# The units of the attention's key tiles as one stream, with one exponential over two units

## The chip, the cores and the metric

The kernel runs on one core of a Trainium2 chip. Its engines are TensorE (PE; its weight loads are listed as PEld), VectorE (DVE), ScalarE (ACT), GpSimd (POOL) and SyncE (SP, which issues DMAs). Each takes its instructions in the order of its own queue and waits for the others through semaphores. PE writes into eight PSUM banks of 128 x 512 fp32 elements; DVE and ACT read them, POOL works in SBUF. The metric is the device time of one launch in microseconds (us), the median of several runs.

## The reference

The input is four images of 128 channels and 64 x 64 positions. A first layer (convolution, state-space scan, norms) is added to it; then each image becomes 4,096 tokens of 128 channels, which go through an additive attention and a recurrent layer. Only the attention is touched here:

```python
q = jnp.einsum('bld,ud->blu', x, Wt)                     # U = 32
k = jnp.einsum('bld,ud->blu', x, Wx)
beta = jnp.tanh(q[:, :, None, :] + k[:, None, :, :] + bh)
alpha = jnp.einsum('bsju,u->bsj', beta, Wa[:, 0]) + ba[0]
alpha = jax.nn.softmax(jnp.tanh(alpha), axis=-1)
c_r = jnp.einsum('bsj,bjd->bsd', alpha, x)               # added to the tokens
```

For each of 4 x 4,096 queries and 4,096 keys this is a sum of 32 hyperbolic tangents, weighted by `Wa`.

## The kernel before

The kernel has three stages: `_layer0`, `_rational` (the attention) and `_chunked` (the recurrent layer). A fourth, `_general`, is entered only if a test on the device fails. All that follows is in `_rational`, whose instructions stand on the engines' queues in the order in which the Python code emits them.

A sum of several tanh terms is a ratio of two sums over sign patterns: with m terms there are 2^m patterns, each an exponential of a signed sum of q's, times one of k's. The 32 terms are split into groups of 6, 6, 5, 5, 5 and 5, so the patterns take 64 + 64 + 32 + 32 + 32 + 32 rows. `F` holds the keys' exponentials (two layers of 128 rows, 4,096 keys), `E` the queries' (512 at a time), and `cE` the queries' times the weights. A denominator is a product of `F` with `E`, a numerator one of `F` with `cE`, each contracting the 64 or 32 rows of its group. A tile of 128 keys and 512 queries so needs six ratios; they are made in three units of two:

- unit A: layer 0, rows 0 to 63 and 64 to 127
- unit B1: layer 1, rows 0 to 31 and 32 to 63
- unit B2: layer 1, rows 64 to 95 and 96 to 127

`products` (L1201) writes a unit's two denominators (`lower`, L1209) into a tile `pd` of two banks, its two numerators (`upper`, L1214) into two tiles `pn` of one bank. There are two `pd` (four banks), three `pn` and one `ct`. In the trace every fp32 product is two passes of a matmul, so it counts as two.

The loop is over four images and eight query blocks of 512 each, 32 blocks in all, and inside over 32 key tiles `jt`. Per tile:

- `inverse` (L1221), ACT: a Ln of the 1,024 denominators (L1223), then an Exp of the negative (L1224), which gives the reciprocals in `ra` (unit A) or `rb` (B1, B2)
- `times` (L1217), DVE: the two halves multiplied by the numerators, from PSUM (L1219)
- POOL: the ratios of B1 added to those of A (L1338), and those of B2 (L1325)
- DVE: the two halves added into `A[:, jt, :]` (L1335)

The order on PE is by hand (L1315 to L1342): denominators of A, numerators of B2 of the tile before beside denominators of B1, numerators of A, denominators of B2 beside numerators of B1. B2's multiplication, its addition and the sum into `A` come one tile late.

After the 32 tiles ACT applies tanh and exp to `A` in four parts (L1373, L1374). Meanwhile the next block's tile 0 is made with DVE's reciprocal instead of ACT (`ahead`, L1355, and `direct`, L1227); so the loop of all blocks but the first starts with tile 1. `weighted` (L1349) multiplies `A` by the transposed tokens `xT` into the bank `ct`; the products of tiles 0 to 19 come at once, those of the last twelve are put between tiles 2 to 13 of the next block. `closing` (L1235) divides and stores: `take`, `den`, four reciprocals and `end`, at the tiles of `CLOSE_AT`. The table `between` also holds the norm of the next image (`NORM_AT`), the next queries (`QUERIES_AT`) and, at an image's start, the transposes `turn`. The keys of the next image are made at the end of an image (L1382).

Of the kernel before, what the change touches and what calls it, by code (L numbers as in the profile page):

```python
# [8 lines left out]
F32 = mybir.dt.float32  # L9
AF = mybir.ActivationFunctionType  # L10
# [5 lines left out]
P = 128  # L16
# [22 lines left out]
WARM = 16  # L39
QB = 512  # L40
PARTS = ((0, 4), (4, 12), (12, 20), (20, 32))
CLOSE_AT = (14, 16, 17, 18, 19, 20, 21)
NORM_AT = (15, 17, 19, 20)
QUERIES_AT = (23, 25)
NOW = 20
REACH = 21.0
LOWER = 2.0**-13
# [1001 lines left out]
def _rational(ctx, tc, k, x1, x2, top, Wt, Wx, bh, Wa, ba):  # L1049
# [11 lines left out]
    one = ctx.enter_context(tc.tile_pool(name="none", bufs=1))  # L1061
    two = ctx.enter_context(tc.tile_pool(name="ntwo", bufs=2))
    sb = ctx.enter_context(tc.tile_pool(name="nsb", bufs=2))
    ra = ctx.enter_context(tc.tile_pool(name="nra", bufs=3))
    rb = ctx.enter_context(tc.tile_pool(name="nrb", bufs=4))
    psD = ctx.enter_context(tc.tile_pool(name="npsD", bufs=2, space=PSUM))
    psN = ctx.enter_context(tc.tile_pool(name="npsN", bufs=3, space=PSUM))
    psW = ctx.enter_context(tc.tile_pool(name="npsW", bufs=1, space=PSUM))
# [7 lines left out]
    def pn():  # L1076
        return psN.tile([P, QB], F32, name="pn", tag="pn")
# [57 lines left out]
    def exponent(ps, w, src, i, out, bias=0.0):  # L1135

        nc.tensor.matmul(ps, w[:, i * P : (i + 1) * P], src, start=True, stop=True)  # L1137
        nc.scalar.activation(out, ps, AF.Exp, bias=bias)
        n = next(tops)
        nc.vector.tensor_reduce(top[:, n : n + 1], ps, AX.X, ALU.max)  # L1140


    def norm_load(b, xn, cols):
        nc.sync.dma_start(xn[:, cols], x1[b, :, cols])

    def norm_steps(xn, cols, alloc):

        xc = xn[:, cols]
        n = cols.stop - cols.start
        held = {}  # L1150

        def centre():
            ps = alloc()
            _mm(nc, ps, k.avg, xc, n)
            nc.vector.tensor_tensor(xc, xc, ps, ALU.subtract)

        def square():
            held["sq"] = rb.tile([P, CH], F32, name="sq", tag="rb")[:, 0:n]
            nc.scalar.activation(held["sq"], xc, AF.Square)

        def rate():
            ps = alloc()
            _mm(nc, ps, k.avg, held["sq"], n)
            _rsqrt(nc, held["sq"], ps, k.eps5)

        def scale():
            nc.gpsimd.tensor_tensor(xc, xc, held["sq"], ALU.mult)

        return centre, square, rate, scale

    def keys(F, xn, c, ps, i):

        exponent(ps, w_k, xn[:, blocks[c]], i, F[:, i, blocks[c]], b_k[:, i : i + 1])

    def turn(xT, xn, c):

# [34 lines left out]
        products((ps[:, 0, :], ps[:, 1, :]), unit, F, jt, E)  # L1211
        return ps

    def upper(unit, F, jt, cE):  # L1214
        return products((pn(), pn()), unit, F, jt, cE)

    def times(r, ns):  # L1217
        for a in range(2):
            nc.vector.tensor_tensor(r[:, a, :], r[:, a, :], ns[a], ALU.mult)  # L1219

    def inverse(d, pool, tag):  # L1221
        r = pool.tile([P, 2, QB], F32, name=tag, tag=tag)
        nc.scalar.activation(r, d, AF.Ln, scale=LOWER)  # L1223
        nc.scalar.activation(r, r, AF.Exp, scale=-1.0)  # L1224
        return r

    def direct(d, ns, pool, tag):  # L1227

        r = pool.tile([P, 2, QB], F32, name=tag, tag=tag)
        for a in range(2):  # L1230
            nc.vector.reciprocal(r[:, a, :], d[:, a, :])  # L1231
            nc.vector.scalar_tensor_tensor(r[:, a, :], r[:, a, :], 1.0 / LOWER, ns[a], ALU.mult, ALU.mult)
        return r

    def closing(b, s, ct, xr, parts):  # L1235

        held = {}

        def take():
            held["ct"] = one.tile([P, QB], F32, name="ct_s")  # L1240
            nc.vector.tensor_copy(held["ct"], ct)

        def denominators():
            held["den"] = pw()
            nc.tensor.matmul(held["den"], den_w, held["ct"], start=True, stop=True)
            held["rec"] = one.tile([P, QB], F32, name="rec")

        def invert(i):
            cols = slice(i * QB // parts, (i + 1) * QB // parts)
            nc.vector.reciprocal(held["rec"][:, cols], held["den"][:, cols])  # L1250

        def end():
            num = pn()
            nc.tensor.matmul(num, fix, held["ct"], start=True, stop=True)
            nc.vector.tensor_tensor(held["rec"], held["rec"], num, ALU.mult)
            nc.gpsimd.tensor_tensor(xr, xr, held["rec"], ALU.add)
            nc.sync.dma_start(x2[b, :, blocks[s]], xr)

        return [take, denominators] + [lambda i=i: invert(i) for i in range(parts)] + [end]


    nn = L // CH
    xn = two.tile([P, L], F32, name="xn")
    for c in range(nn):
        norm_load(0, xn, slice(c * CH, (c + 1) * CH))
    ln_exp()
    todo = [
        norm_steps(xn, slice(c * CH, (c + 1) * CH), lambda: pd().rearrange("p a q -> p (a q)")) for c in range(nn)
    ]
    for i in range(nn + 1):  # L1270
        for d, c in ((0, i), (1, i), (2, i - 1), (3, i - 1)):
            if 0 <= c < nn:
                todo[c][d]()
    F = big.tile([P, 2, L], F32, name="F")
    xT = big.tile([P, JT, P], F32, name="xT")
# [16 lines left out]
    for b in range(B):  # L1292
        upcoming = None
        for s in range(nq):
# [16 lines left out]
                        lambda i=i, s=s, of=of, E_next=E_next: queries(E_next, of, (s + 1) % nq, i)  # L1311
                    )
            ln_exp()
            late = None
            for jt in range(start, JT + 1):  # L1315
                if jt < JT:
                    dA = lower("A", F, jt, E) if jt > start else first[0]
                if late is not None:
                    pj, rA_, rB2_ = late
                    nB2 = upper("B2", F, pj, cE)  # L1320
                if jt < JT:
                    dB1 = lower("B1", F, jt, E) if jt > start else first[1]
                if late is not None:
                    times(rB2_, nB2)
                    nc.gpsimd.tensor_tensor(rA_, rA_, rB2_, ALU.add)  # L1325
                if jt < JT:
                    nA = upper("A", F, jt, cE)
                    rA = inverse(dA, ra, "ra")
                    times(rA, nA)
                    dB2 = lower("B2", F, jt, E)  # L1330
                    nB1 = upper("B1", F, jt, cE)
                    rB1 = inverse(dB1, rb, "rb")
                    times(rB1, nB1)
                if late is not None:
                    nc.vector.tensor_tensor(A[:, pj, :], rA_[:, 0, :], rA_[:, 1, :], ALU.add)  # L1335
                if jt == JT:
                    break
                nc.gpsimd.tensor_tensor(rA, rA, rB1, ALU.add)  # L1338
                rB2 = inverse(dB2, rb, "rb")
                late = jt, rA, rB2  # L1340
                for go in between.pop(jt, ()):
                    go()  # L1342

            if more:
                E, cE = E_next, weigh(E_next)
# [9 lines left out]
            def ahead(step):  # L1355
                if not more:
                    return
                if step == 0:
                    held["A"], held["B1"] = lower("A", F, 0, E), lower("B1", F, 0, E)
                    held["A"] = direct(held["A"], upper("A", F, 0, cE), ra, "ra")  # L1360
                elif step == 1:
                    held["B2"] = lower("B2", F, 0, E)
                    held["B1"] = direct(held["B1"], upper("B1", F, 0, cE), rb, "rb")
                    nc.gpsimd.tensor_tensor(held["A"], held["A"], held["B1"], ALU.add)
                elif step == 2:
                    held["first"] = lower("A", F, 1, E)
                    r = direct(held["B2"], upper("B2", F, 0, cE), rb, "rb")
                    nc.gpsimd.tensor_tensor(held["A"], held["A"], r, ALU.add)
                else:
                    held["first"] = held["first"], lower("B1", F, 1, E)  # L1370

            for i, (lo, hi) in enumerate(PARTS):
                nc.scalar.activation(A[:, lo:hi, :], A[:, lo:hi, :], AF.Tanh, bias=b_a)  # L1373
                nc.scalar.activation(A[:, lo:hi, :], A[:, lo:hi, :], AF.Exp)  # L1374
                if i == 0:
                    if turned:

                        F = big.tile([P, 2, L], F32, name="F")
                        for c in range(nq):
                            ps = pd()  # L1380
                            for a in range(2):
                                keys(F, upcoming, c, ps[:, a, :], a)  # L1382
                    ahead(0)
                if hi <= NOW or not more:
                    for jt in range(lo, hi):
                        weighted(jt)
                ahead(i + 1) if i + 1 < len(PARTS) else None
            if more:
                nc.vector.tensor_tensor(A[:, 0, :], held["A"][:, 0, :], held["A"][:, 1, :], ALU.add)
                first = held["first"]  # L1390
                start = 1
            between = {}
# [207 lines left out]
```

## Time and profile before

| | |
|---|---|
| median of three runs | 11853.89 us (11846.7 to 11861.68) |
| profiled execution | 11853.99 us |
| its span, first to last instruction | 11852.3 us |
| PE, DVE, ACT, POOL busy in the span | 88%, 78%, 80%, 73% |
| instructions of the attention | from 4071 to 11550 us |
| one query block without a change of image (6189.3 to 6417.9) | 228.6 us; ACT busy 221.3, PE 222.6, DVE 171.7, POOL 162.5 |
| one with a change of image (5926.4 to 6189.3) | 262.9 us; ACT busy 232.6 |
| Ln of 1,024 columns from PSUM | 1.01 to 1.03 us |
| Exp of 1,024 columns in SBUF | 1.06 us |
| multiplication, 512 columns (L1219) | 0.68 us |
| POOL's additions, 1,024 columns (L1325, L1338) | 2.37 and 2.65 us |

A row of the page's groups, or of the trace's, gives the source line, the engine, the tile written and the tiles read, the shape, the count, the busy time and the mean in nanoseconds; behind the second bar stands how long the engine was idle just before these instructions and what ended most of that. A row of the timeline gives start and duration; rows that follow each other on an engine are merged and counted. A busy PE is not one at its peak: its matmuls overlap, and their ends are modelled.

### The profile page before, as it was taken

Reading aid. Unit: us, or ns where it says so; the run is one execution under the profiler, and the core shown is the slowest. Engines: PE = TensorE matmul, PEld = TensorE weight load, DVE = VectorE, ACT = ScalarE, POOL = GpSimd, SP = SyncE. Lnnn points to the kernel's source line nnn. Section 1 sums busy time; section 2 is a strip of 40 time slices with the busy share of each in tenths; the row PEclk is TensorE's granted clock in tenths of the full one; section 3 lists DMA queues with packets and bytes.
Section 4 is the critical chain, followed back from the end, with each engine's and each line's share of the span. In section 5 each row is a group of like instructions: output and inputs, shape, how many; then the busy total and the mean of one; then the engine's idle time right before and its main releaser. Section 6 shows DMA issues by size and latency. Waiting matters only on the chain.

```text
span 11852.3 us, 111573 instructions
## 1 busy us (share of the span) xinstructions
PE 10379.5 (88%) x36083; PEld 3211.2 (27%) x36083; DVE 9191.1 (78%) x10131; ACT 9444.7 (80%) x10096; POOL 8602.6 (73%) x3648
## 2 busy tenths in 40 slices
PE   6687787678677699999999999999999999999996
PEld 2121122122111133333333333323333323333324
DVE  4999899899989677777777777777777767777763
ACT  3455555655555599999989999989999989999985
POOL 2899889889889677677757776767677667767761
PEclk8898898899888799999999999999999999999998
DMA  4778778778778300000000000000000000000001
GB/s 105 181 178 197 170 173 190 177 174 189 176 170 182 78 1 6 3 3 3 6 3 3 3 6 3 3 6 3 3 3 6 3 2 2 4 2 2 4 15 46
DMA packets 224900, 737.81 MB, mean 62 GB/s; under 512 B 41057, under 2 KB 42017, under 8 KB 223793
## 3 DMA queue, kind: packets, MB, share of 16 engines
q1 hardware_dynamic: 221184, 729.96, 26.1%
q8 instruction: 284, 4.65, 0.2%
q14 instruction: 312, 2.55, 0.1%
q10 hardware_dynamic: 3120, 0.64, 0.0%
HBM read 613.01 MB, written 117.44 MB: 62 GB/s over the span
## 4 chain that ended last, share of the span: by engine, by line
PE 48%; ACT 11%; DVE 4%; issue 3%; POOL 2%; DMA 0%; POOLq 0%; DVEq 0%; SPq 0%; ACTq 0%
PE pn L1204 25%; PE pd L1204 15%; ACT A L1373 4%; PE ct L1349 3%; ACT A L1374 2%; DVE rb L1219 1%; ACT rb L1223 1%; ACT rb L1224 1%; PE ct L1137 1%; DVE A L1335 1%; ACT ra L1223 1%; POOL ra L1338 1%; POOL ra L1325 1%; PE wxs L1492 0%; PE pd L1137 0%
## 5 line engine op out<-in xcount | busy, mean ns | idle before, releaser
L1204 PE MATMUL pn<-cE,F 32*128 32x512 f32 (+1 forms) x12288 | 4740.0, 651 | 174.3 <-DVE cE L1192 58.0
L1219 DVE TENSOR_TENSOR rb<-rb,pn 128x512 f32<-128x512 f32 x3972 | 2546.0, 682 | 1310.2 <-PE pd L1204 683.5
L1204 PE MATMUL pd<-E,F 32*128 32x512 f32 (+1 forms) x12288 | 3507.2, 654 | 33.8 <-DVE ra L1231 32.2
L1338 POOL TENSOR_TENSOR ra<-ra,rb 128x1024 f32<-128x1024 f32 x993 | 2634.6, 2653 | 960.3 <-DVE rb L1219 960.3
L1325 POOL TENSOR_TENSOR ra<-ra,rb 128x1024 f32<-128x1024 f32 x993 | 2348.5, 2365 | 381.1 <-DVE rb L1219 320.3
L629 POOL TENSOR_TENSOR dBu<-dtdu,bbcc 128x1024 f32<-128x1024 f32 x1024 | 2397.6, 2366 | 276.6 <-DMA dtdu<-ddd 158.4
L1224 ACT ACTIVATE rb<-rb 128x1024 f32<-128x1024 f32 x1986 | 2103.2, 1059 | 62.8
L1204 PEld LDWEIGHTS pn<-cE,F 32*128 32x128 f32 (+1 forms) x12288 | 1424.6, 185 | 2560.7 <-DVE rb L1219 995.7
L1223 ACT ACTIVATE rb<-pd 128x1024 f32<-128x1024 f32 x1986 | 2009.0, 1012 | 100.5 <-PE pn L1204 87.7
L671 PE MATMUL py<-h,gather 128*32 128x512 f32 x4096 | 1298.7, 698 | 478.2 <-POOL h L654 381.5
L1219 DVE TENSOR_TENSOR ra<-ra,pn 128x512 f32<-128x512 f32 x1986 | 1316.5, 684 | 234.6 <-ACT ra L1224 196.8
L1204 PEld LDWEIGHTS pd<-E,F 32*128 32x128 f32 (+1 forms) x12288 | 936.5, 186 | 1673.6 <-issue 751.2
L624 ACT ACTIVATE pa<-dtdu,a_neg 128x1024 f32<-128x1024 f32 x1024 | 1147.2, 1120 | 52.2 <-DVE h L644 31.3
L654 POOL TENSOR_TENSOR h<-h,bbcc 128x1024 f32<-128x1024 f32 x384 | 923.0, 2404 | 343.3 <-ACT carry L652 336.7
L644 DVE TENSOR_TENSOR_SCAN pa<-pa,carry,dBu 128x1024 f32<-128x1024 f32 x480 | 1125.8, 2345 | 22.3 <-ACT pa L624 11.3
L1224 ACT ACTIVATE ra<-ra 128x1024 f32<-128x1024 f32 x993 | 1050.9, 1058 | 31.4
L1349 PE MATMUL ct<-A,xT 128*128 128x512 f32 x2048 | 1037.1, 633 | 10.3 <-ACT A L1374 10.1
L1223 ACT ACTIVATE ra<-pd 128x1024 f32<-128x1024 f32 x993 | 1010.0, 1017 | 44.1 <-PE pd L1204 10.7
L652 ACT COPY carry<-pa 128x1 f32<-128x1 f32 x640 | 103.6, 162 | 1118.3 <-DVE h L651 1116.5
L1335 DVE TENSOR_TENSOR A<-ra 128x512 f32<-128x512 f32 x993 | 749.8, 755 | 114.6 <-POOL ra L1325 114.6
L651 DVE TENSOR_TENSOR h<-pa,bbcc 128x1024 f32<-128x1024 f32 x640 | 784.1, 1225 | 60.4 <-DVE pa L644 1.8
L644 DVE TENSOR_TENSOR_SCAN h<-pa,carry,dBu 128x1024 f32<-128x1024 f32 x288 | 675.1, 2344 | 115.4 <-PE py L671 70.7
(286 smaller groups left out, 8847.9 us busy)
## 6 DMA issues: line engine op xcount, KB each, us to landing
bbcc<-bcd SPq DMA_DIRECT2D x1024, 256.0 KB, 7.0
dtdu<-ddd SPq DMA_DIRECT2D x1024, 256.0 KB, 7.1
ddd<-dd SPq DMA_DIRECT2D x64, 1024.0 KB, 5.1
src<-src SPq DMA_DIRECT2D x64, 512.0 KB, 8.3
xs<-in_x_dram SPq DMA_DIRECT2D x16, 512.0 KB, 7.6
src<-xs SPq DMA_DIRECT2D x16, 512.0 KB, 3.0
bcd<-bc SPq DMA_DIRECT2D x64, 128.0 KB, 2.0
src<-xsT SPq DMA_DIRECT2D x16, 512.0 KB, 4.4
```

What stands on the lines that cost most here:

```text
L624: nc.scalar.activation(dA, its[m].DT[r][:, 0, :], AF.Exp, scale=a)
L629: nc.gpsimd.tensor_tensor(dBu, its[m].DT[r][:, 1, :], its[m].BC[q][:, 0, :], ALU.mult)
L644: nc.vector.tensor_tensor_scan(to[:, step], dA[:, step], live.pop(("dBu", u))[:, step], 0.0 if m % nch == 0 else its[m - 1].carry[:, col : ...
L654: nc.gpsimd.tensor_tensor(h, h, cc, ALU.mult)
L671: nc.tensor.matmul(it.y[to, c], gather, live["h", v][:, c], start=False, stop=(q == QS - 1))
L1204: nc.tensor.matmul(ps[a], F[lo:hi, i, jt * P : (jt + 1) * P], side[lo:hi, i, :], start=True, stop=True)
L1219: nc.vector.tensor_tensor(r[:, a, :], r[:, a, :], ns[a], ALU.mult)
L1223: nc.scalar.activation(r, d, AF.Ln, scale=LOWER)
L1224: nc.scalar.activation(r, r, AF.Exp, scale=-1.0)
L1325: nc.gpsimd.tensor_tensor(rA_, rA_, rB2_, ALU.add)
L1338: nc.gpsimd.tensor_tensor(rA, rA, rB1, ALU.add)
L1349: nc.tensor.matmul(ct, xT[:, jt, :], A[:, jt, :], start=(jt == 0), stop=(jt == JT - 1))
```

## The change

The tiles' units become one stream: `units` lists A, B1, B2 of all the block's tiles, and a loop takes two of them at a time, without regard to where a tile ends. The two share a buffer `r` of 2,048 columns: each has its own Ln, and one Exp covers both. `upper` makes one half of a unit's numerators at a time, into one bank. On PE the numerators of the units in hand alternate with the denominators of the units four and five places ahead. On DVE, a sum into `A` stands between two multiplications; on POOL, the additions of the pair follow each other. What is in `between` for a tile is emitted in the round before the one that holds the tile's B2.

Besides: the keys of a new image are made by `all_keys`, two products, then two Exps, then two maxima; the first norms work on 512 columns in `pn` banks; the squares of the norm have their own two buffers; the last product of `closing` uses the `ct` bank; and two positions in `CLOSE_AT` and `QUERIES_AT` move by one tile. The pools `ra` (3) and `rb` (4), of 1,024 columns, give way to `rr` (4), of 2,048.

```diff
-CLOSE_AT = (14, 16, 17, 18, 19, 20, 21)
+CLOSE_AT = (14, 16, 17, 18, 19, 20, 22)
-QUERIES_AT = (23, 25)
+QUERIES_AT = (24, 26)
...
-    ra = ctx.enter_context(tc.tile_pool(name="nra", bufs=3))
-    rb = ctx.enter_context(tc.tile_pool(name="nrb", bufs=4))
+    rr = ctx.enter_context(tc.tile_pool(name="nrr", bufs=4))
...
+    def all_keys(F, xn, c):
+        ps = pd()
+        for i in range(2):
+            nc.tensor.matmul(ps[:, i, :], w_k[:, i * P : (i + 1) * P], xn[:, blocks[c]], start=True, stop=True)
+        for i in range(2):
+            nc.scalar.activation(F[:, i, blocks[c]], ps[:, i, :], AF.Exp, bias=b_k[:, i : i + 1])
+        for i in range(2):
+            n = next(tops)
+            nc.vector.tensor_reduce(top[:, n : n + 1], ps[:, i, :], AX.X, ALU.max)
...
-    def upper(unit, F, jt, cE):
-        return products((pn(), pn()), unit, F, jt, cE)
+    def upper(unit, F, jt, cE, half):
+        ps = pn()
+        i, parts = groups[unit]
+        lo, hi = parts[half]
+        nc.tensor.matmul(ps, F[lo:hi, i, jt * P : (jt + 1) * P], cE[lo:hi, i, :], start=True, stop=True)
+        return ps
...
         def end():
-            num = pn()
+            num = pw()
...
-            late = None
-            for jt in range(start, JT + 1):
...
+            units = [(jt, unit) for jt in range(start, JT) for unit in ("A", "B1", "B2")]
+            den, num, ratio = dict(enumerate(first)), {}, {}
+            sums = []
...
+            def inverses(u):
+                pair = [v for v in (u, u + 1) if v < len(units)]
+                if not pair:
+                    return
+                r = rr.tile([P, 2, 2, QB], F32, name="r")
+                for i, v in enumerate(pair):
+                    ratio[v] = r[:, i]
+                    nc.scalar.activation(r[:, i], den.pop(v), AF.Ln, scale=LOWER)
+                n = len(pair)
+                nc.scalar.activation(r[:, 0:n], r[:, 0:n], AF.Exp, scale=-1.0)
+
+            def times(u, half):
+                if u < len(units):
+                    r = ratio[u][:, half, :]
+                    nc.vector.tensor_tensor(r, r, num.pop((u, half)), ALU.mult)
+
+            def added(u):
+                if u >= len(units) or units[u][1] == "A":
+                    return
+                to = ratio[u - (1 if units[u][1] == "B1" else 2)]
+                nc.gpsimd.tensor_tensor(to, to, ratio[u], ALU.add)
+                if units[u][1] == "B2":
+                    sums.append((units[u][0], to))
+
+            def summed():
+                for jt, r in sums:
+                    nc.vector.tensor_tensor(A[:, jt, :], r[:, 0, :], r[:, 1, :], ALU.add)
+                sums.clear()
+
+            inverses(0)
+            numerators(0, 0)
+            numerators(0, 1)
+            denominators(2)
+            numerators(1, 0)
+            denominators(3)
+            for u in range(0, len(units), 2):
+                inverses(u + 2)
+                times(u, 0)
+                numerators(u + 1, 1)
+                denominators(u + 4)
+                times(u, 1)
+                numerators(u + 2, 0)
+                denominators(u + 5)
+                times(u + 1, 0)
+                numerators(u + 2, 1)
+                summed()
+                times(u + 1, 1)
+                added(u)
+                added(u + 1)
+                for v in (u + 2, u + 3):
+                    if v < len(units) and units[v][1] == "B2":
+                        for go in between.pop(units[v][0], ()):
+                            go()
+                numerators(u + 3, 0)
+            summed()
```

`denominators(u)` calls `lower`, and `numerators(u, half)` calls `upper`, for the unit `u` of the stream if there is one.

## The prediction

> **What bounds the kernel now.** I read the page first (busy shares, slices, the chain that ended last), then the stage of the change by windows, by form, and instruction by instruction.
>
> ```profile
> span 11852.3 us, 111573 instructions
> ACT  3455555655555599999989999989999989999985
> PE 48%; ACT 11%; DVE 4%; issue 3%; POOL 2%; DMA 0%; POOLq 0%; DVEq 0%; SPq 0%; ACTq 0%
> ```
>
> ```profile
> 6189.30:6417.90 228.60, 222.62 (x845) 69.86 (x844) 171.66 (x241) 221.26 (x202) 162.47 (x67) 0.97 0.01 4
> ```
>
> The span stands against the profiled execution's own 11853.99 us, 0.1 above the median of the runs, 11853.89. The slices show ACT at 8 to 9 tenths in the attention alone; in the chain PE leads. The last line is one of 32 query blocks (PE, PEld, DVE, ACT, POOL busy): PE and ACT are both near 97%, so the profile of busy time cannot say which sets the pace. The order of single instructions can:
>
> ```profile
> 6000.30 1.12 PE L1349 MATMUL ct<-A,xT 128*128 128x512 f32 x2
> ...
> 6001.35 1.13 PE L1204 MATMUL pd<-E,F 64*128 64x512 f32 x4
> ...
> 6002.41 0.70 PE L1204 MATMUL pn<-cE,F 32*128 32x512 f32 x2
> ...
> 6002.43 0.70 PE L1204 MATMUL pd<-E,F 32*128 32x512 f32 x2
> ...
> 6003.48 2.02 PE L1204 MATMUL pn<-cE,F 64*128 64x512 f32 x4
> 6003.59 1.06 ACT L1224 ACTIVATE ra<-ra 128x1024 f32<-128x1024 f32 x1
> 6003.64 1.28 DVE L1219 TENSOR_TENSOR rb<-rb,pn 128x512 f32<-128x512 f32 x2 [1.36 <-PE pd L1204]
> ...
> 6005.44 0.70 PE L1204 MATMUL pd<-E,F 32*128 32x512 f32 x2
> ...
> 6005.45 0.82 PE L1204 MATMUL pn<-cE,F 32*128 32x512 f32 x2
> ...
> 6006.63 0.30 PEld L1349 LDWEIGHTS ct<-A,xT 128*128 128x128 f32 x2 [0.76 <-issue]
> 6006.63 1.13 PE L1349 MATMUL ct<-A,xT 128*128 128x512 f32 x2
> ```
>
> This is one key tile with a closing product (ct): 6.33 us, and PE has no gap. A product holds its quarters of the rows for one turn of 1.06 us (two passes; 6001.35 to 6002.41), also when it uses 32 rows. Products on other quarters share a turn: B2's numerators and B1's denominators at 6002.41. And PE keeps its order: the pn at 6005.45 could run from 4.98 (its rows were free, its bank came back with the multiplication begun at 6004.25), but stands behind the pd at 6005.44, which waited for rows 64 to 128. So a tile costs 4 turns, 5 with ct, plus 0.9 where A's second numerator waits for a bank. Without ct the same tile takes 6.01 (Ln to Ln of A, 5902.25 to 5908.26), with ACT back to back: there ACT paces.
>
> The price of an Exp by its width, from the groups by form:
>
> ```profile
> L1224 ACT ACTIVATE rb<-rb 128x1024 f32<-128x1024 f32 x1823 | 1930.6, 1059 | 57.6
> ...
> L1374 ACT ACTIVATE A<-A 128x2048 f32<-128x2048 f32 x29 | 55.4, 1912 | 0.9
> ```
>
> Of how DVE and GpSimd meet, from the timeline:
>
> ```profile
> 6353.27 2.36 POOL L1338 TENSOR_TENSOR ra<-ra,rb 128x1024 f32<-128x1024 f32 x1
> 6353.36 2.82 DVE L1335 TENSOR_TENSOR A<-ra 128x512 f32<-128x512 f32 x1 [0.42 <-POOL ra L1325]
> ```
>
> The tile's last sum, both operands in SBUF, asks while GpSimd adds: it ends 0.55 after the addition, in 2.82 instead of 0.69.
>
> By the sums (L1335) the block 6189 to 6418 divides into an edge of 38.5 (6193.94 to 6232.45: tanh, exponentials, the first tile), 12 tiles with ct in 75.9 (to 6308.33), and 18 others in 114.2 (to 6422.56).
>
> **ACT.** Two units start to start cost 4.01 now (6.01 x 2/3). After: Ln to Ln 0.91 (1.01 less the 0.10 overlap seen between independent ACT instructions), Ln to dependent Exp 1.04, Exp of 2048 to Ln 1.82 (1912 less 0.10): 3.77. It saves 0.24 on each of 1,489 pairs, 357 us of ACT, worth nothing where ACT doesn't pace; its cover is the PE order below, and if that gave way the 357 would be gained. The joint Exp also waits for the second Ln, so a pair's first ratio comes 0.9 later; behind it in ACT's queue stand only the next pair's Ln. The Trainium skill, "ScalarE: Activation LUTs", section What ACT_TABLE_LOAD costs, has a fixed 186 ns per ACTIVATE and 93 ns overlap; by it the saving would be 0.19 a pair, an estimate of 277 us; the rows decide for 0.24.
>
> **PE.** No product is added, but the order is new, and I walked the emitted order by turns. Write n and d for numerator and denominator, a and b for halves, primes for later tiles, quarters in brackets. Two tiles are three loop rounds: nB1b(1) dB1'(0,1) nB2a(2) dB2'(2,3) nB2b(3) [ct] nA'a(01); nA'b(23) dA''(01,23) nB1'a(0) dB1''(0,1) nB1'b(1) [ct] nB2'a(2); nB2'b(3) dB2''(2,3) nA''a(01) dA'''(01,23) nA''b(23) nB1''a(0). A unit's denominators (two tiles' units ahead) now stand next to numerators of the same kind of unit, so on the same quarters, and the one order lets nothing pass. With each product in the first turn that its quarters and the order allow, the starts without ct are: 0 nB1b; 1 dB1', nB2a; 2 dB2'; 3 nB2b, nA'a; 4 nA'b, dA'' on (01); 5 dA'' on (23), nB1'a; 6 dB1''; 7 nB1'b, nB2'a, nB2'b; 8 dB2'', nA''a; 9 dA'''; 10 nA''b, nB1''a and the next nB1b. That is 10 turns where before there were 8. A ct needs all quarters and parts nB2b from nA'a, nB1'b from nB2'a: 2 turns each, so 14, where before there were 10. 14 x 1.06 = 14.84; and once in it the three banks run out: from a product to its multiplication 1.16, to the bank's return 0.72, less the turn of 1.06 that passes anyway, 0.82 (bounds 0 and twice that). Two ct tiles: 15.66, against 12.66.
>
> **The other tiles.** PE's 10.6 and ACT's 3 x 3.77 = 11.3 would both be under 12.02. But DVE's queue now mixes the sum between multiplications, and the two additions of a round go to GpSimd together. An addition starts 0.83 after its multiplication; the next sum asks 1.20 after that same one, so it waits out 2.36 - 0.37 and takes 0.45 more: 2.44. Behind it stand the multiplication (0.72), which the next addition awaits (0.11 + 2.38), the sum that awaits that (0.60), the multiplication behind it that frees a bank (0.72), four PE turns (4.24), the product's way to DVE (1.16), and two multiplications (1.20) before the next sum: 13.57 for two tiles. That loop is unseen in the trace of before; if no sum met an addition it would be 11.73, if both did, 15.41. I take 13.57, as the order has just one meeting. Nine such rounds: 122.1, plus what DVE does besides (take 0.6, four reciprocals 0.87 each, the product with rec 0.6, xn 0.6, two maxima 1.2: 6.5) and six other products (den, num, two norms, two queries: 6.4) in the same loop: 135.0.
>
> For this wait the Trainium skill has "SBUF — State Buffer", section SBUF: two separate sides: the port pair that DVE and GpSimd share is an exclusive lock for a whole instruction. It speaks against the change: by it every sum could stand up to a full addition, an estimate of 31 x 2.3 = 71 us a block. In the trace of before 912 sums lost only 912 x (0.754 - 0.687) = 61 us in all.
>
> **Small parts.** The edge: the first ratio now needs two Ln and an Exp of 2048 (3.9 against 2.1), and one more loop round passes before the first sum: 1.8 + about 3 = 5. Bounds 0 and 10. Keys of the next image: Exps and maxima now overlap the products, 30 us becomes about 18, three times: -36; the turns of the image (8 DVE copies and 8 groups of transposes, 1.8 each, now inside the loop): +43. These and the prologue's eight norms instead of four I set at 0 (bounds -40 and +60). The closing product with `fix` moves from the pn banks to the ct bank (same turn, one bank fewer in the ring's way), the queries and the last closing step go one tile later, and the squares get buffers of their own: I cost these at nothing, since each is issued the same number of times, inside the loop whose price stands above; if the ct bank were still held when `fix` asks, PE would stand for the rest of a multiplication, 0.7 a block, 22 us. The four more loads of the first norms stand on SP's queue before anything else of the stage (bounds 0 and 10).
>
> **Sum.** Per block: ct tiles 6 x 15.66 - 75.9 = +18.1; others 135.0 - 114.2 = +20.8; edge +5: +43.9. Times 32: +1,405. On 11,854: 13,260 us.
>
> **Rivals.**
> ACT paces, so the change does what its words say (the other side): PE would have to fill free quarters past a blocked product and no sum may meet an addition. Rounds of 11.31: 6 x (11.31 - 12.66) + 9 x (11.31 - 12.02) + 5 = -9.5, times 32 = -304: 11,550. It decides when a round averages under 12.3. The pn held at 6005.45 speaks against it; 0.04.
> PE overtakes but the port loop stays: ct rounds 13.57, 5.5 + 20.8 + 5 = 31.3, 12,855; 0.10.
> PE keeps order, but GpSimd is idle when sums ask: 9 x 11.73 + 12.9 = 118.5, so 18.1 + 4.3 + 5 = 27.4, 12,730. For it: before, nearly all sums found it idle. 0.13.
> Both sums meet additions: 9 x 15.41 + 12.9 = 151.6, 60.5 a block, 13,790; 0.10.
> No measurable change, gains and losses cancelling: 0.01.
>
> **How the numbers follow.** The forecast has 0.62, and with its bounds (turn 1.04 to 1.07, edge 0 to 10) reaches 13,000 to 13,560. The range 12,720 to 13,600 takes in the two rivals below it, 0.85. A change under 0.2% (24 us) could not be told from none: faster 0.04, same 0.01, slower 0.95.
>
> **What would show it.** Right: blocks of about 272 us; ct sums in pairs 15.7 apart; ACT near 80% in the block with idle time ended by PE pd; PE waiting for DVE; sums of 2.5 us in plain rounds. Wrong: d and n on different quarters starting out of order, or ACT still at 97%.

## The result

The changed kernel takes 12,566.35 us (median of 4 runs, 12,556.12 to 12,574.22), the kernel before 11,857.61 on the same chip: 1.0597 times as long, 95% interval 1.0583 to 1.0611, 709 us slower. The prediction had 13,260. The sign is right, the size nearly twice what came.

The page of the kernel after: the span, ScalarE's row of the slices, and the shares of the chain that ended last.

```profile
span 12567.5 us, 107276 instructions
...
ACT  3455555555555688888888888888888888888884
...
PE 40%; DVE 17%; POOL 6%; ACT 3%; issue 3%; DMA 0%; POOLq 0%; DVEq 0%; SPq 0%; ACTq 0%
```

The profiled execution took 12,569.45 us. ScalarE has gone from 8 and 9 tenths to 8 in nearly every slice of the attention, and VectorE and GpSimd, 4% and 2% of the chain before, are 17% and 6%. One block after, by windows (PE, PEld, DVE, ACT, POOL busy, then the clock):

```profile
5914.01:6163.14 249.13, 234.57 (x846) 95.07 (x845) 187.04 (x242) 212.96 (x155) 153.64 (x66) 0.95 0.01 4
```

228.6 us have become 249.1. By the tiles' last sums (line 1353, before line 1335), mean of the 27 blocks without a change of image:

| part of a block, us | before | after | difference | predicted |
|---|---|---|---|---|
| edge | 38.5 | 43.3 | +4.8 | +5 |
| 12 tiles with a closing product | 75.9 | 75.9 | 0.0 | +18.1 |
| 18 other tiles | 113.9 | 129.6 | +15.7 | +20.8 |

The sums are taken by their starts, as in the prediction. By their ends the second and third rows after are 77.4 and 127.8, since the sum at the border between them is one that waits.

The span is 715 us longer: 624 in the 31 blocks from the first tanh on, 71 in the first block (209.4 before, 280.2 after, first exponential to first tanh), 10 in the norms and keys ahead of it, 6.5 ahead of the stage and 4 behind it, where nothing is changed.

Two stretches carry the reading. First TensorE in two tiles with closing products (start, duration, product, rows):

```profile
5728.59 0.69 PE L1228 MATMUL pn<-cE,F 64*128 64x512 f32 x1
5728.60 0.69 PE L1214 MATMUL pd<-E,F 64*128 64x512 f32 x1
...
5730.51 1.59 PE L1228 MATMUL pn<-cE,F 32*128 32x512 f32 x5
...
5731.47 1.02 PE L1214 MATMUL pd<-E,F 32*128 32x512 f32 x4
...
5733.61 1.13 PE L1388 MATMUL ct<-A,xT 128*128 128x512 f32 x2
5734.67 1.13 PE L1228 MATMUL pn<-cE,F 64*128 64x512 f32 x4
5735.63 1.02 PE L1214 MATMUL pd<-E,F 64*128 64x512 f32 x4
5736.59 0.69 PE L1228 MATMUL pn<-cE,F 32*128 32x512 f32 x1
...
5738.51 1.13 PE L1388 MATMUL ct<-A,xT 128*128 128x512 f32 x2
5739.56 1.13 PE L1228 MATMUL pn<-cE,F 32*128 32x512 f32 x4
5740.53 1.02 PE L1214 MATMUL pd<-E,F 32*128 32x512 f32 x4
5741.48 0.69 PE L1228 MATMUL pn<-cE,F 64*128 64x512 f32 x1
```

Products of one height now stand together: 64 rows, 32 rows, a closing product of 128, and so on. From 5728.59 to 5741.48 that is 12.89 us with no gap, in groups of one height that last 1.92, 3.10, 1.06, 1.92, 1.92, 1.05 and 1.92 (the row at 5730.51 is from a window that begins there; in a longer one it is merged with the 64-row products ahead of it); from the numerators at 5734.67 to the denominators of the same rows it is 0.96, not 1.06. Next, the meeting in a plain round:

```profile
5850.08 2.35 POOL L1347 TENSOR_TENSOR r<-r 128x1024 f32<-128x1024 f32 x1
...
5850.45 2.52 DVE L1353 TENSOR_TENSOR A<-r 128x512 f32<-128x512 f32 x1
...
5852.90 2.57 DVE L1340 TENSOR_TENSOR r<-r,pn 128x512 f32<-128x512 f32 x4
5853.07 1.94 ACT L1333 ACTIVATE r<-pd 128x1024 f32<-128x1024 f32 x2 [3.10 <-DVE A L1353]
...
5856.12 0.69 DVE L1353 TENSOR_TENSOR A<-r 128x512 f32<-128x512 f32 x1 [0.65 <-POOL r L1347]
```

The sum asks at 5850.45, GpSimd's addition ends at 5852.43, the sum at 5852.97; the multiplications stand behind it. ScalarE, idle for 3.10, starts 0.10 after the sum's end: its next logarithm writes into one of the four buffers `r`, the one that this sum reads. The round's second sum, at 5856.12, meets nothing. What sets the pace of such a round is the chain, here in a later block (start, duration; the rows left out are more products of TensorE and stretches without a wait on record):

```profile
6923.41 1.70 DVE A L1353
...
6925.80 0.69 DVE r L1340
6926.61 2.38 POOL r L1347
...
6929.63 0.69 DVE r L1340
6930.36 1.29 PE pn L1228 x3
...
6934.97 1.26 DVE r L1340 x2
6936.23 1.71 DVE A L1353
```

A sum that waits, a multiplication, the addition, a multiplication that frees a bank, TensorE's products, two multiplications, and the next sum: 12.82 us, and ScalarE is not on it; whether a fifth buffer would change anything was not tried. The page sums it up (busy, mean ns | idle before):

```profile
L1333 ACT ACTIVATE r<-pd 128x1024 f32<-128x1024 f32 x2979 | 2950.3, 1017 | 972.7 <-DVE A L1353 421.7
...
L1353 DVE TENSOR_TENSOR A<-r 128x512 f32<-128x512 f32 x993 | 1255.7, 1265 | 285.2 <-POOL r L1347 285.0
```

A sum takes 1,265 ns on the mean, 755 before; 993 of them above 0.69 make 570 us of waiting, 65 before.

### The profile page after: what moved, and what is told of

Its sections match the earlier page's. It is cut to its first block, busy times and chain, and to the rows that moved or that the text cites. A ratio compares the mean times of both kernels' runs of the same rounds, so it can differ in the third digit from the quotient of the medians.

```text
span 12567.5 us, 107276 instructions
## 1 busy us (share of the span) xinstructions
PE 10812.4 (86%) x36083; PEld 4026.0 (32%) x36083; DVE 9708.8 (77%) x10135; ACT 9173.8 (73%) x8634; POOL 8310.8 (66%) x3652
## 4 chain that ended last, share of the span: by engine, by line
PE 40%; DVE 17%; POOL 6%; ACT 3%; issue 3%; DMA 0%; POOLq 0%; DVEq 0%; SPq 0%; ACTq 0%
PE pn L1228 20%; PE pd L1214 14%; DVE r L1340 6%; DVE r L1234 5%; POOL r L1347 5%; DVE A L1353 3%; PE ct L1388 3%; DVE r L1235 1%; ACT r L1335 1%; PE ct L1136 1%; ACT r L1333 1%; POOL r L1404 1%; PE wxs L1530 0%; PE pn L55 0%; DVE top L1139 0%
## 5 line engine op out<-in xcount | busy, mean ns | idle before, releaser
L1347 POOL TENSOR_TENSOR r<-r 128x1024 f32<-128x1024 f32 x1986 | 4688.9, 2361 | 2277.4 <-DVE r L1340 2132.2
L1228 PE MATMUL pn<-cE,F 32*128 32x512 f32 (+1 forms) x12288 | 5262.8, 657 | 401.2 <-DVE r L1340 305.4
L1340 DVE TENSOR_TENSOR r<-r,pn 128x512 f32<-128x512 f32 x5958 | 3855.9, 681 | 1149.6 <-PE pn L1228 804.6
L1214 PE MATMUL pd<-E,F 32*128 32x512 f32 (+1 forms) x12288 | 4652.7, 635 | 82.7 <-DVE r L1234 68.5
L1333 ACT ACTIVATE r<-pd 128x1024 f32<-128x1024 f32 x2979 | 2950.3, 1017 | 972.7 <-DVE A L1353 421.7
L1335 ACT ACTIVATE r<-r 128x2048 f32<-128x2048 f32 (+1 forms) x1505 | 2849.1, 1893 | 47.8
L1214 PEld LDWEIGHTS pd<-E,F 32*128 32x128 f32 (+1 forms) x12288 | 1816.2, 192 | 1313.7 <-issue 1029.7
L1353 DVE TENSOR_TENSOR A<-r 128x512 f32<-128x512 f32 x993 | 1255.7, 1265 | 285.2 <-POOL r L1347 285.0
L644 DVE TENSOR_TENSOR_SCAN pa<-pa,carry,dBu 128x1024 f32<-128x1024 f32 x480 | 1125.2, 2344 | 22.7 <-ACT pa L624 11.3
L1234 DVE RECIPROCAL r<-pd 128x512 f32<-128x512 f32 x186 | 623.3, 3351 | 76.7 <-POOL r L1404 76.7
L1413 ACT ACTIVATE A<-A,b_a 128x4096 f32<-128x4096 f32 (+2 forms) x128 | 473.3, 3697 | 0.4
```

The lines of the kernel that those rows point to most:

```text
L644: nc.vector.tensor_tensor_scan(to[:, step], dA[:, step], live.pop(("dBu", u))[:, step], 0.0 if m % nch == 0 else its[m - 1].carry[:, col : ...
L1214: nc.tensor.matmul(ps[a], F[lo:hi, i, jt * P : (jt + 1) * P], side[lo:hi, i, :], start=True, stop=True)
L1228: nc.tensor.matmul(ps, F[lo:hi, i, jt * P : (jt + 1) * P], cE[lo:hi, i, :], start=True, stop=True)
L1333: nc.scalar.activation(r[:, i], den.pop(v), AF.Ln, scale=LOWER)
L1335: nc.scalar.activation(r[:, 0:n], r[:, 0:n], AF.Exp, scale=-1.0)
L1340: nc.vector.tensor_tensor(r, r, num.pop((u, half)), ALU.mult)
```

## The experiments

**What a product costs, by itself.** If the two tiles of the first stretch were the 14 turns of the prediction, they would have taken 14.8 us and a wait. So first the turn:

```diff
+    # halves alone, in turn
+    for i in range(16):
+        nc.tensor.matmul(q[2 * (i % 2)], *rows(64 * (i % 2), 64), start=True, stop=True)
...
+    # one quarter four times, then the next
+    for i in range(16):
+        nc.tensor.matmul(q[i // 4], *rows(32 * (i // 4), 32), start=True, stop=True)
```

> The whole computation is left out, and zeros are written; what is left are products of 512 columns with nothing to wait for, in seven series, and two series of GpSimd additions (1024 columns) beside VectorE operations (512 columns). Theory of turns (the prediction's): a product holds its quarters for 1.06 us whatever stands before it, and none passes another: 16 halves in turn take 8 x 1.06 = 8.5 us, 16 quarters in turn 4.2 us, one quarter four times and then the next 13 x 1.06 = 13.8 us. Theory of heights: a product takes two passes of 0.43, 0.86 us, and only a change between 32, 64 and 128 rows adds some 0.2 us; products on free quarters may pass: halves in turn 6.9 us, quarters in turn 3.4 us, a pair of halves and a pair of quarters 1.06 us each, a half and a quarter of the other rows never together, and one quarter four times and then the next between 3.4 us (all pass) and 11.2 us (none does). VectorE: with both operands in SBUF eight operations beside GpSimd's additions take far more than 8 x 0.6 us; with one operand in PSUM they take 8 x 0.6 us, if the wait is for SBUF's port; both the same, if it is for anything else.

Its timeline on TensorE; each series ends where the separating products (line 85) start. Line 90: 16 halves in turn; 94: 16 quarters in turn; 99: pairs of halves and pairs of quarters by turns; 104: a pair of halves, a whole; 113: one quarter four times, then the next.

```profile
45.56 7.14 PE L90 MATMUL q<-m,w 64*128 64x512 f32 x32
52.63 3.70 PE L85 MATMUL q<-m,w 128*128 128x512 f32 x8
56.26 3.71 PE L94 MATMUL q<-m,w 32*128 32x512 f32 x32
59.91 3.70 PE L85 MATMUL q<-m,w 128*128 128x512 f32 x8
63.54 8.54 PE L99 MATMUL q<-m,w 64*128 64x512 f32 x32
72.00 3.70 PE L85 MATMUL q<-m,w 128*128 128x512 f32 x8
75.63 12.76 PE L104 MATMUL q<-m,w 64*128 64x512 f32 x36
88.23 3.60 PE L85 MATMUL q<-m,w 128*128 128x512 f32 x8
...
107.87 9.18 PE L113 MATMUL q<-m,w 32*128 32x512 f32 x32
116.98 3.70 PE L85 MATMUL q<-m,w 128*128 128x512 f32 x8
```

Halves in turn take 7.07 us for eight turns, 0.86 each and 0.2 once at the end; quarters 3.65 for four. With a change of height after every pair it is 8.46 for eight: 1.06 each. So the turn of 1.06 is 0.86 of work and 0.2 for a change of height, and the whole and the pair of halves (12.60 for twelve turns) pay it as well. The series on line 113 takes 9.11 us: in strict order it would be 13 products one behind another, 11.2, so products on a free quarter pass others of their height. The theory of turns is refuted on both counts. In the last series (line 118, not shown above) a half and a quarter of other rows start 1.05 us apart, one after the other, as long as the clock is full: a free quarter helps only a product of the same height.

**Do the closing products cost 18 us a block?**

```diff
-                nc.tensor.matmul(ct, xT[:, jt, :], A[:, jt, :], start=(jt == 0), stop=(jt == JT - 1))
+                nc.tensor.matmul(ct, xT[:, jt, :], A[:, jt, :], start=(jt == 0), stop=(jt == (NOW if more else JT) - 1))
...
-                    between[2 + i] = [lambda jt=jt, weighted=weighted: weighted(jt)]
+                    between[2 + i] = []
```

> The kernel after without the twelve closing products of each block that stand between the key tiles (31 blocks; the sum over the keys then lacks these tiles). Theory of turns (the prediction's): each costs two turns of 1.06 us of the array, 25 us a block, 790 us in all: below 11,900. Theory of heights: each costs some 0.6 us of the array (rounds of two tiles of 12.90 with closing products against 11.65 without, in the run with the sums on GpSimd), and in the kernel after this lies beside the loop of VectorE and GpSimd, since the plain rounds take 12.81 as well: 0 to 30 us gained, 12,535 to 12,570.

Measured: 12,545.70 us, 1.0591 of before (1.0575 to 1.0608) where the kernel after has 1.0597: 372 closing products are worth 7 us by the ratios, 21 by the medians. The rounds of two tiles go from 12.90 to 12.82. The chain shows what takes over when they are gone:

```profile
PE 29%; DVE 23%; POOL 9%; issue 4%; ACT 3%; DMA 0%; POOLq 0%; DVEq 0%; SPq 0%; ACTq 0%
```

TensorE's 12.9 and the ring of VectorE and GpSimd, 12.8, are two limits that lie almost level, so taking one away gives nothing.

**Do the sums set the plain rounds?** Once without the sum, once with the sum on GpSimd behind the addition that it needs:

```diff
-                for jt, r in sums:
-                    nc.vector.tensor_tensor(A[:, jt, :], r[:, 0, :], r[:, 1, :], ALU.add)
```

> The kernel after without the sum of the two halves into A (A is filled with zeros once); all products, logarithms, exponentials, multiplications and GpSimd additions stay. If the sums that wait behind GpSimd's additions set the rounds: plain rounds fall from 12.81 to ScalarE's 11.3, 9 x 1.5 = 13.5 us a block, and the edge gives back about 2; rounds with a closing product stay near 12.8 if there TensorE sets them: 12,070 to 12,140 us. If they fell as well, 9 us a block more, 11,800. If TensorE's order sets all rounds (the prediction's theory, its turns mis-sized): no more than 60 us gained, 12,500 or more.

```diff
                 if units[u][1] == "B2":
-                    sums.append((units[u][0], to))
+                    if True:
+                        nc.gpsimd.tensor_tensor(A[:, units[u][0], :], to[:, 0, :], to[:, 1, :], ALU.add)
...
```

> The kernel after with the sum of the two halves given to GpSimd, behind the addition that it needs: VectorE then has no operation with both operands in SBUF in the loop, GpSimd has 512 columns more a tile, by half of 2.36 us some 1.2, so 5.9 us a tile. If the meeting of sum and addition sets the rounds: as without the sum, 12,070 to 12,170. If GpSimd's load of additions is what the loop waits for: slower than the kernel after, 12,700 or more. If TensorE's order sets them: 12,500 to 12,600.

Measured: 12,263.39 us without the sum (1.0349, 1.0331 to 1.0366) and 12,196.52 with it on GpSimd (1.0294, 1.0277 to 1.0311): 303 and 370 us less than the kernel after (294 and 359 by the ratios), though GpSimd has more to do in the second. The page of the second:

```profile
L1347 POOL TENSOR_TENSOR r<-r 128x1024 f32<-128x1024 f32 x1986 | 4698.4, 2366 | 740.3 <-DVE r L1340 636.5
...
L1333 ACT ACTIVATE r<-pd 128x1024 f32<-128x1024 f32 x2979 | 2962.3, 1016 | 619.1 <-PE pn L1228 464.1
...
L1350 POOL TENSOR_TENSOR A<-r 128x512 f32<-128x512 f32 x993 | 1264.9, 1274 | 77.9
```

ScalarE's idle time before the logarithms falls from 972.7 to 619.1, and VectorE's sum no longer stands at its end. Plain rounds take 11.65 us (3.77, 3.97 and 3.91 from one joint exponential to the next), rounds with closing products still 12.90. So the meeting is some half of the loss. The other half is not taken apart by a run: with the sums on GpSimd a block without a change of image still takes 236.4 us on the mean, 228.3 before, and the first block 273, 209 before. Both runs stayed above what was expected, by 123 and 27 us: the rounds fell to 11.65, not to ScalarE's 11.3, and the tiles with other work stayed long. That leaving the sum out gains less than moving it is not settled; part may be the clock (from the first exponential to the last tanh TensorE has half the clock for some 550 us there, 440 with the sum on GpSimd).

**Is the joint exponential worth anything here?**

```diff
-                n = len(pair)
-                nc.scalar.activation(r[:, 0:n], r[:, 0:n], AF.Exp, scale=-1.0)
+                for i in range(len(pair)):
+                    nc.scalar.activation(r[:, i], r[:, i], AF.Exp, scale=-1.0)
```

> The kernel after with two exponentials of 1024 columns in the place of the joint one of 2048. If ScalarE paces anywhere, a pair costs 0.2 us more there: on all 1,489 pairs +300 us, 12,870. If GpSimd, VectorE or TensorE set the rounds, the joint exponential is worth nothing: 12,540 to 12,600, the same within 0.3%; the first ratio of a pair then comes no earlier, since the second logarithm still stands ahead of both.

Measured: 12,568.94 us (1.0601, 1.0584 to 1.0619), the same. As the prediction had it, the shorter exponential is worth nothing in this order of work, since ScalarE waits.

**The first block and the laden tiles.** Here the run with the sums on GpSimd still takes 273 us for the first block. Its timeline around one of the keys' products:

```profile
4184.40 1.12 PE L1228 MATMUL pn<-cE,F 32*128 32x512 f32 x2
...
4185.45 1.13 PE L1136 MATMUL ct<-xn,w_k 128*128 128x512 f32 x2
...
4187.33 0.69 DVE L1139 TENSOR_REDUCE top<-ct 128x1 f32<-128x512 f32 x1 [2.39 <-ACT F L1137]
4187.94 2.58 DVE L1340 TENSOR_TENSOR r<-r,pn 128x512 f32<-128x512 f32 x4
```

The numerator at 4184.40 waits for a bank that a multiplication gives back, the keys' product stands behind it, the maximum waits for the keys, and the next round's multiplications stand behind the maximum: a ring. If it costs what it seems to, calling these steps earlier opens it (a list of its own keeps the closing products at the round's end):

```diff
                 times(u, 1)
+                for v in (u + 2, u + 3):
+                    if v < len(units) and units[v][1] == "B2":
+                        for go in between.pop(units[v][0], ()):
+                            go()
...
-                    between[2 + i] = [lambda jt=jt, weighted=weighted: weighted(jt)]
+                    closed[2 + i] = [lambda jt=jt, weighted=weighted: weighted(jt)]
```

> As the run with the sums on GpSimd, and the keys, queries, norms, turns and closing steps called in the middle of a round, behind the second multiplication, instead of at its end (the closing products stay at the end). At the end the product of such a step stands on TensorE behind a numerator that waits for the third multiplication, and its maximum on VectorE stands ahead of the next round's multiplications: a ring, rounds of 6 to 7.8 us instead of 4.35. If that ring is what the first block (273 us against 209 before) and the laden tiles lose: the first block back to about 225, a block 2 to 5 us shorter: 12,000 to 12,090. If these steps cost what they are (the product, the exponential, the maximum) wherever they stand: within 30 us of 12,197.

Measured: 12,181.12 us (1.0284, 1.0268 to 1.0300), only some 12 to 16 us less: the total speaks for the rival. The rounds tell more. From one joint exponential to the next, two neighbouring rounds of the first block take 4.96 and 6.33 us at full clock, where in the run with the sums on GpSimd rounds of the same kind took 6.12 and 7.06; but the second to the fourth take 7.34, 7.69 and 8.40, with passes of 1.06 us instead of 0.59 in most of their time. Over the 28 blocks without a change of image I took, place by place, the intervals between joint exponentials in which passes ran at half clock, less the median of the same place at full clock: 237 us here, 83 in the run with the sums on GpSimd. So the ring is there and opening it gains at full clock; by this measure the clock took most of the gain. That is not shown beyond the measure: at one place 27 of the 28 intervals are at half clock here, so that the value at full clock rests on one, and whether the clock fell because TensorE waited or the other way round was not tested. How much of the first block's 71 us is the ring alone stays open; in that block the granted clock is 0.98 before and 0.90 after.

**The closing products two by two.**

```diff
+                if u % 6 == 0:
+                    for at in sorted(closed):
+                        if (at, "B2") in units[: u + 4]:
+                            for go in closed.pop(at):
+                                go()
```

> As the run before it, and the closing products of two tiles stand next to each other, once in three rounds. If the change of height is the price of a closing product, a pair saves one change there and back, some 0.2 to 0.3 us a pair, 6 pairs and 31 blocks: 40 to 60 us less than the run before it. If the price is the product alone: the same within 15 us. Sum for the kernel: 11,950 to 12,080.

Measured: 12,118.65 us (1.0230, 1.0214 to 1.0246), 62 less than the run before it on the same chip. A pair takes 1.91 us of the array (twice 0.86 and one change), two single ones 2.12; 0.2 on 6 pairs in 31 blocks is 37 us. From one joint exponential to the next, two tiles with closing products take 12.77 us (3.77, 5.09 and 3.91) where they took 12.90, which is 24 us in all. The half clock is less here too (113 us by the same measure, 237 there), so the rest need not be the closing products'. The kernel before is still faster by 273.

**The clock, and VectorE beside GpSimd.**

```diff
+    # one quarter alone
+    for i in range(24):
+        nc.tensor.matmul(q[0], *rows(0, 32), start=True, stop=True)
...
+    for i in range(8):
+        nc.gpsimd.tensor_tensor(g, g2, s, ALU.add)
+    for i in range(8):
+        nc.vector.tensor_tensor(d, s[:, 0, :], z, ALU.mult)
```

> The whole computation is left out, and zeros are written. Products of 512 columns without a wait, 20 us and more of one kind, between series of whole ones (128 rows); and eight VectorE operations beside GpSimd's additions, once with both operands in SBUF and once with one in PSUM. In the run with the closing steps called earlier a block lost 8.5 us in intervals whose passes took 1.06 us instead of 0.59, though TensorE was hardly idle. If the clock follows idle time alone, no series here slows: a pass stays at 0.43 us everywhere. If it follows how many rows are at work, one quarter alone (a fourth of the rows) and a half in turn with a quarter of the other rows fall to half the clock within 10 us, the pairs do not, and one half alone lies between. VectorE beside GpSimd: 19.9 us for eight in SBUF as before; if the wait is for SBUF's port, 5 to 6 us with PSUM; if it is GpSimd itself that slows VectorE, 15 us or more.

The slices' clock, and the timeline: line 92 one quarter alone, 96 one half alone, 100 two quarters, 105 a half and a quarter of other rows, 110 pairs; VectorE with both operands in SBUF (117) and with one in PSUM (124), beside GpSimd's additions (115 and 122).

```profile
PEclk9999999965555699999999999855555569999999
```

```profile
46.70 36.39 PE L92 MATMUL q<-m,w 32*128 32x512 f32 x48
94.91 20.86 PE L96 MATMUL q<-m,w 64*128 64x512 f32 x48
126.20 20.87 PE L100 MATMUL q<-m,w 32*128 32x512 f32 x96
157.50 44.96 PE L105 MATMUL q<-m,w 64*128 64x512 f32 x48
214.33 25.47 PE L110 MATMUL q<-m,w 64*128 64x512 f32 x96
...
6.83 19.90 DVE L117 TENSOR_TENSOR d<-s 128x512 f32<-128x512 f32 x8
30.59 5.74 DVE L124 TENSOR_TENSOR d<-s,z 128x512 f32<-128x512 f32 x8 [0.93 <-POOL g L118]
...
5.92 23.01 POOL L115 TENSOR_TENSOR g<-g,s 128x1024 f32<-128x1024 f32 x8 [5.48 <-DVE g L77]
30.64 19.35 POOL L122 TENSOR_TENSOR g<-g,s 128x1024 f32<-128x1024 f32 x8
```

TensorE is busy throughout, and the clock halves all the same: 5.5 us into the products on one quarter, and 3 us into those in turn on a half and a quarter of the rows. With half of the rows at work it stays. So in these five series the clock follows how much of the array works. Eight VectorE operations take 19.90 us beside the additions with both operands in SBUF, 5.74 with one in PSUM: the wait belongs to operations on SBUF alone, and GpSimd pays too (23.0 instead of 19.35). The first experiment had the same pair, 19.89 and 5.74.

**One part alone, in the kernel before.**

```diff
...
-                            ps = pd()
-                            for a in range(2):
-                                keys(F, upcoming, c, ps[:, a, :], a)
+                            all_keys(F, upcoming, c)
```

> The kernel before with one part of the change alone: at a change of image both keys of a chunk are multiplied first, then both exponentials, then both maxima. By the prediction's small parts 12 us less at each of three changes, -36 us: 11,800 to 11,830. If the edges hide it: the same within 15 us.

Measured: 11,809.89 us against 11,845.81, 0.9968 (0.9957 to 0.9979): faster than both kernels. In the profiled executions the three blocks with a change of image take 15 to 17 us less each (263.0, 259.9 and 261.0 became 246.3, 244.8 and 244.6), 48 in all; the medians differ by 36, and the interval of the ratio allows 25 to 51.

## Why the prediction was wrong, and where it was right

Of the 694 us between the 13,260 that it forecast and the 12,566 measured, 579 are one term, +18.1 a block for the tiles with closing products; the step behind it is the one on a product's turn, two paragraphs below.

**Edge, +5: right in size** (+4.8; its two parts were not measured apart). **ScalarE's 357 us, worth nothing: right**, by the run with two exponentials. **Plain rounds: mechanism right.** It had one sum in two meet an addition and take 2.44; it takes 2.52 to 2.54, and the other 0.69. The round came out at 13.57 and is 12.81 (7.13 and 5.68 from sum to sum). The term that was too large is "four PE turns (4.24)": at 0.86 each they are 3.44, and the round is 12.77. In the round whose chain stands above, the part ahead of TensorE's turns, from the start of the sum (6923.33 in the timeline) to the bank's return (6930.32), is 6.99, and the prediction has 6.97; the rest, to the start of the next sum (6936.15), is 5.83 where it has 6.60. Its estimate of up to 71 us a block, if every sum waited out an addition, came to 18 (570 in all).

**"A product holds its quarters of the rows for one turn of 1.06 us" and "PE keeps its order": wrong**, and with them the 14 turns and the +18.1, which came to 0.0. The groups of the two tiles above are two, three, one, two, two, one and two products one behind another, 13 and not 14, and 7 changes of height: 13 x 0.86 + 7 x 0.2 = 12.6, and 0.3 of waits. In the tiles of the trace before, every turn but one (A's second numerator, held by its bank) came after one of another height, so the price of the neighbourhood was taken for the price of the product. The edge of the same trace had the other price, eight closing products in a row on TensorE, 0.86 each:

```profile
5981.33 7.13 PE L1349 MATMUL ct<-A,xT 128*128 128x512 f32 x16
```

The row that the prediction read as strict order was the change of height as well: the 32-row numerator at 6005.45 started when the 64-row products begun at 6003.48 had left the array, and by the first experiment no free quarter would have let it in sooner. The rule is in the Trainium skill, "TensorEngine Tiling (Array Packing)", Tiling Modes, Key Properties: changing the tiling mode, not just the tile, drains the engine. The first experiment agrees, with 0.2 us a change. The new order, which put like units side by side, had fewer changes (7 in two tiles, where before a tile had 5), which the prediction read as the reverse, products in each other's way.

**VectorE's other work and six other products in plain rounds, +12.9: near.** The 18 tiles came to 129.6 where 135.0 was forecast; with the round corrected to 12.77 the same sum gives 127.8.

**Small parts at 0: wrong for the first block.** The sum counts that block like the others, with 43.9, though it has no closing products and no edge; it lost 71. The keys of this block were costed as in the edges alone; inside the loop they, their maxima and TensorE form the ring. The keys at the change of image, -36, are right by themselves (36 less), but inside the change the three blocks gain only some 3 us each on the others. The prediction puts the turns of the image "now inside the loop"; that is a misreading, since `between` holds them in both kernels, and their copies run between the tiles before (6132.6 to 6177.2) as after (6362.6 to 6431.2). What changed is what they cost there: the 18 tiles with them take 2 us more than the others' before, 13 more after, and that takes most of the 14 that the edges gain on the others.

Of the signs that it named, ScalarE's idle time and sums of 2.5 us in plain rounds came; blocks of 272 us (249), sums 15.7 apart in tiles with closing products (12.9) and ScalarE near 80% of the block (213 of 249, 85%) did not. The rival that had TensorE pass and the port's loop stay (12,855) came nearest to the case; it was 290 us too high by the turn of 1.06 in that loop and by rounds of 13.57 with closing products.

## What to carry to other kernels

Before a turn of an engine is priced, look for a stretch where the neighbours are alike: a price read only where the kind changes every time contains the change. Where products use parts of the array's rows, put those of one height together and pair the whole ones. An operation that reads and writes SBUF alone, placed on VectorE in front of work that others await, costs the rest of the GpSimd addition that it meets, and everything behind it waits too; where GpSimd has room, it may do that operation itself (370 us here).

## What the runs showed of the hardware beyond that

The clock halved with TensorE never idle, when a quarter of the rows, or a half and a quarter in turn, were at work; at half of the rows it stayed. The Trainium skill, "TensorE: Matmul & The Clock Gate", Part 1, tells of a gate that opens with activity and closes after an idle window of about 3.4 us. The run shows that thin products close it too, after 3 to 5.5 us. In the kernels half clock cost, by the measure above, 78 us before, 105 after, and 237 in the run with the steps called early. That measure holds only the rounds of the 28 blocks. From the first exponential to the last tanh TensorE has half the clock for some 430 us before and 860 after (a mean clock of 0.97 and 0.95); what that cost in the first block, at the edges and at the changes of image was not measured, so the clock may be a part of the loss that the experiments leave open.
